# A pair begun in every step from step 165 on, chunks of two from batch 44, narrower load waits, allotment in pieces, fills over two steps

## The chip, the cores and the metric

The kernel runs on one core of a Trainium2 chip. A core has five engines that each work through their own list of instructions in order: PE (TensorE, matrix products), DVE (VectorE), ACT (ScalarE), POOL (GpSimd) and SP (SyncE, which here only issues transfers). The metric is the time of one execution on the device in microseconds; less is better.

## The reference

64 batches of 256 tokens, each of 256 numbers, go through two layers. The first is a graph attention with four heads and a linear layer; the second a graph attention with one head and a mixture of eight experts of which each token uses two. Each part is added to its input:

```
x = x + L0_gnn(layernorm(x), adj)        # 4 heads of 64, masked softmax over 256 nodes, elu
x = x + layernorm(x) @ weight.T + bias
x = x + L1_gnn(layernorm(x), adj)        # 1 head of 256, relu
t = layernorm(x)
rw, re = top_k(softmax(t @ router_w.T), 2); rw = rw / rw.sum()
x = x + t + sum over e of combine[:, e] * (gelu(t @ w1[e] + b1[e]) @ w2[e] + b2[e])
```

All arithmetic is in 32-bit floats.

## The kernel before

A batch is two tiles of 128 tokens. `batch_layers(b, ...)` carries one batch through both attentions and the linear layer, up to the router's logits. The last three batches (61 to 63) are computed **densely**: `route_dense` finds their two weights per token, and `dense_expert` runs each of the eight experts over all their tokens. The first 61 are **routed**: they are gathered into chunks, and when the last batch of a chunk is done, `route` does the following for the whole chunk.

1. `top_two` finds each token's two experts, and two matmuls (L1099, L1100) with a running sum give every token-expert couple a row in that expert's region of a table in HBM, `xs`. This is a chain of small DVE operations.
2. `allot` decides from the counts how many blocks of 256 rows (a **pair**, two tiles) are full in each expert's region, and which expert and which block each of the next `n` pairs takes. It is a generator in five pieces, 19 DVE operations in all (L833 to L870). `in_one` runs all the pieces at once; `spread`, true for chunks of four batches, takes one piece in each of four steps.
3. `send` scatters the rows of each tile to `xs`, twice, once for each expert (L1056, indirect transfers issued by POOL).
4. The pairs are put into the list `waiting`.

After the last chunk, `allot` is called once more for the blocks that are not full (`FLUSH` = 14 pairs), and eight **fills** (L1168, issued by SP) write harmless rows behind each expert's last row.

`expert_pair` is one pair: four loads of its rows from `xs` into `xr` (L892), one of four further numbers per row into `xt` (L903), one of the expert's weights into `we` (L917); DVE turns the rows into `sT` (L117); `hidden` multiplies with the first weights (`ph`, L950) and applies gelu; `result` multiplies with the second (`py`, L965), DVE adds the bias (`y`, L975), and ACT scales each row (L943). Then `scatter` adds the two tiles of `y` to the output with two indirect transfers from POOL (L986). Rows of different pairs can be the same token, so both adds of a pair wait until the two adds of the pair before have landed.

What a load waits for: `xs` is one tensor, so a load of it waits for every earlier write of `xs`, sends and fills alike, that nothing has waited for yet. It also waits explicitly for the transfers in `needs`, the sends of its own chunk (or the fills). Sends and fills themselves are exempt from waiting for loads and for each other (the group "rows").

The order of all instructions is written by the loop at the end of the function. It counts **steps**, three to a batch (`TICKS` = 3); batch b begins at step 3b. In each step every active generator is advanced to its next `yield`, in the order of the numbers that they yielded last, smaller first; a negative number means once more in the same step. Up to step 176 two pairs are begun in every third step; from `DRAIN_AT` (step 177) on, one in each step, as long as fewer than three results wait for `scatter`. One `scatter` is issued per step. A dense expert's job is begun as soon as it is ready, one per step for the first dense batch and one per two steps for the other two. The same constant `DRAIN_AT` also sets one number of `batch_layers`, which the change leaves alone. The last store, of batch 63, waits for all the adds (`store_dense`, L1031).

Of the kernel before, what the change touches and what calls it, by code (L numbers as in the profile page):

```python
# [17 lines left out]
SYNC = mybir.DependencyQuery.ANY_SYNC  # L18
# [9 lines left out]
def kernel(  # L28
# [18 lines left out]
    B, N, D = x.shape  # L47
# [4 lines left out]
    NT = N // P  # L52
# [4 lines left out]

    CHUNKS = (4,) * 12 + (2,) * 5 + (1,) * 3  # L60
    ROUTED = sum(CHUNKS)
    DENSE = B - ROUTED
    assert DENSE > 0
# [298 lines left out]

    half_done = []
    DRAIN_AT = TICKS * (B - 5)
    order, order_steps = [], []

    def norm_stats(src):
# [407 lines left out]
    def in_one(parts):  # L775

        got = None
        for got in parts:
            pass
        return got  # L780
# [95 lines left out]
    def expert_pair(j, n, ids, ef, regs, needs):  # L876

        i = j % GROUP
        upto = min(j + GROUP, n)
        if i == 0:  # L880
            _, regs["e"] = nc.values_load_multi_w_load_instructions(
                ids[0:1, 0, j:upto], engines=[mybir.EngineType.SP], min_val=0, max_val=E - 1,
                skip_runtime_bounds_check_because=WHY,
            )
            _, regs["t"] = nc.values_load_multi_w_load_instructions(
                ids[0:1, 1, j:upto], engines=[mybir.EngineType.SP], min_val=0, max_val=E * CAP,
                skip_runtime_bounds_check_because=WHY,
            )
        e_sp, t_sp = regs["e"][i], regs["t"][i]
        xr = io.tile([P, PAIR // S, KT * S], F32, tag="xr", name="xr", bufs=XBUFS)  # L890
        loads = [
            nc.sync.dma_start(  # L892
                out=xr[g * S : (g + 1) * S],
                in_=xs_d.rearrange("(t c q) f -> t q c f", c=PAIR // S, q=S)[
                    bass.ds(t_sp, 1), :, :, g * KT * S : (g + 1) * KT * S
                ].rearrange("t q c f -> (t q) c f"),
            )
            for g in range(P // S)
        ]

        xt = small.tile([P, 2, ROW - D], F32, tag="xt", name="xt", bufs=14)
        loads.append(
            nc.sync.dma_start(  # L903
                out=xt,
                in_=xs_d.rearrange("(t k p) c -> t p k c", p=P, k=2)[
                    bass.ds(t_sp, 1), :, :, D:
                ].rearrange("t p k c -> (t p) k c"),
            )
        )
        for load in loads:  # L910
            tc.add_to_no_dep_group("rows", load.ins)
            for name in needs:
                tc.add_manual_dep(
                    load.ins, name, AFTER, reason="any sent row may lie in the pair"
                )
        we = io.tile([P, WROW], F32, tag="we", name="we", bufs=WBUFS)
        nc.sync.dma_start(  # L917
            out=we, in_=wpack[bass.ds(e_sp, 1), :, :].rearrange("e p c -> (e p) c")
        )
        yield 90  # L920

        yield 95 if more else 75
        xT = turned(work.tile([P, KT, PAIR], F32, tag="sT", name="sT", bufs=3), xr)
        w = small.tile([P, 2], F32, tag="w", name="w", bufs=12)
        yield 30
        yield 30
        hT = hidden(xT, we)
        yield -65
        nc.vector.scalar_tensor_tensor(
            w[:, :, None], xt[:, :, 1:2], ef[:, j : j + 1], xt[:, :, 2:3],  # L930
            op0=ALU.is_equal, op1=ALU.mult,
        )
        nc.vector.tensor_tensor(w[:, :, None], w[:, :, None], xt[:, :, 3:4], ALU.add)
        yield 80
        if i == 0:
            _, regs["x"] = nc.values_load_multi_w_load_instructions(
                ids[0:1, 0, j:upto], engines=[mybir.EngineType.PE, mybir.EngineType.DVE],
                min_val=0, max_val=E - 1, skip_runtime_bounds_check_because=WHY,
            )
        y = result(hT, bass.ds(regs["x"][i], 1))  # L940
        yield 2
        for t in range(2):
            nc.scalar.activation(y[:, t, :], y[:, t, :], AF.Copy, scale=w[:, t : t + 1])  # L943
        scatters.append((y, xt))
# [109 lines left out]
    def send(xe, at):  # L1054

        d = nc.gpsimd.indirect_dma_start(  # L1056
            out=xs_d[: E * CAP * PAIR, :],
            out_offset=bass.IndirectOffsetOnAxis(ap=at, axis=0), in_=xe, in_offset=None,
        )
        tc.declare_no_dep(  # L1060
            d.ins, query=SYNC, group="rows", reason="sent rows are all different, and none is in a full pair"
        )
        tc.add_to_no_dep_group("rows", d.ins)
        sent.append(d.ins.name)
        nc.gpsimd.nop()

    def later(rank, *phases):
# [5 lines left out]
    def route(c, row0, nt, n, last, xng, lg):  # L1073
# [60 lines left out]
        for i, xe in enumerate(xng):  # L1134
            vec.tensor_copy(xe[:, :, D + 1 :], tail[:, i * NT : (i + 1) * NT, :])
        parts = allot(c, n, False)
        if n and not spread:
            ids, ef = in_one(parts)
        if last:
            ends_at = rt([E], "ends_at", 2, I32)  # L1140
            vec.tensor_copy(ends_at, rows[0])
# [2 lines left out]
        for t in range(nt):  # L1144
            for k in range(2):
                send(xng[t // NT][:, t % NT, :], pos[:, k, t : t + 1])
            if n and spread and t in (1, 2, 4, 5):
                ids, ef = next(parts) or (None, None)
            if not last:
                yield 95  # L1150
            elif t % 2:
                yield 95
        needs = sent[mark:]
        if n:
            regs = {}
# [2 lines left out]
            )  # L1158
        if last:
            parts = allot(c + 1, FLUSH, True)  # L1160
            ids2, ef2 = in_one(parts)
            _, ends_sp = nc.values_load_multi_w_load_instructions(
                ends_at[0:1, :], engines=[mybir.EngineType.SP], min_val=0,
                max_val=(E * CAP - 1) * PAIR, skip_runtime_bounds_check_because="rows of a region",
            )
            filled = []
            for e in range(E):
                d = nc.sync.dma_start(  # L1168
                    out=xs_d[bass.ds(ends_sp[e], PAIR), :].rearrange("(p t) c -> p t c", t=2),
                    in_=fill,  # L1170
                )
                tc.declare_no_dep(
                    d.ins, query=SYNC, group="rows", reason="filling rows lie behind an expert's last row"
                )
                tc.add_to_no_dep_group("rows", d.ins)
                filled.append(d.ins.name)
                nc.sync.nop()
            yield 95
            regs2 = {}
            waiting.extend(  # L1180
                lambda j=j: expert_pair(j, FLUSH, ids2, ef2, regs2, filled)
                for j in range(FLUSH)
            )
# [53 lines left out]
    with tc.manual_schedule():  # L1237
        while more or active or waiting or dense_jobs or scatters:
            phase = step % TICKS
            if more and (phase == 0 or step == 2):  # L1240
                nxt = next(batches, None)
                more = nxt is not None
                if more:
                    begin(nxt, 40 if phase == 0 else 25)
            if step >= SETUP_AT and setup:
                begin(setup.pop(0)(), 90)
            if step >= DRAIN_AT:
                if waiting and len(scatters) < 3:
                    begin(waiting.pop(0)(), 90)
            elif phase == 1:  # L1250
                credit = min(credit + 3.0, 2.0)
                while waiting and credit >= 1.0:
                    credit -= 1.0
                    begin(waiting.pop(0)(), 90)
            if dense_jobs and step >= dense_free:
                units, job = dense_jobs.pop(0)
                dense_free = step + units
                begin(job(), 90)
            if scatters:
                def one():  # L1260
                    scatter()
                    return
                    yield
                begin(one(), 97)
            order_steps.append(step)
            queue = [(a[0], a[1], a) for a in active]
            heapq.heapify(queue)
            while queue:
                *_, entry = heapq.heappop(queue)
                entry[0] = next(entry[2], None)  # L1270
                if entry[0] is not None and entry[0] < 0:
                    entry[0] = -entry[0]
                    heapq.heappush(queue, (entry[0], entry[1], entry))
            if half_done:
                finish_norms(NT)
            if half_squared:
                finish_squares()
            active[:] = [a for a in active if a[0] is not None]
            step += 1
# [35 lines left out]
```

## Time and profile before

| | |
|---|---|
| median of 3 runs | 1519.05 us (1517.03 to 1519.11) |
| profiled execution | 1516.68 us |
| its span, first to last instruction | 1514.9 us |
| granted TensorE clock, mean | 0.985 |
| busy: PE, PEld, DVE, ACT, POOL | 1421.4, 1261.2, 1245.9, 1017.4, 875.8 us |
| indirect adds L986 | 258, 1604 ns each |
| indirect sends L1056 | 244, 1089 ns each |
| matmuls of the experts, L950 and L965 | 1032 + 192 and 1224 |
| loads of `xr`, `xt`, `we` (pairs) | 516, 129, 129 |

PEld is the loading of weights into TensorE, which runs beside its products. A busy engine is one that executes an instruction; waiting and the issuing of transfers do not count. [...] In a line of the timeline come the start and the duration in microseconds, engine, line, operation, what is written and read, and in brackets the idle time of the engine before it and what ended that.

### The profile page before, as it was taken

The page shows a single profiled execution, that of the slowest core. Times are in us where ns is not written, and L with a number is a line of the kernel's source. Part 1 is how long each engine was busy: PE and PEld are TensorE (multiplying, and loading weights), DVE is VectorE, ACT ScalarE, POOL GpSimd, SP SyncE. Part 2 cuts the span into 40 slices and gives each one's busy share as a digit, 9 for nine tenths or more (in the row PEclk, how much of TensorE's full clock was granted, in tenths as well). Part 3 has the DMA queues.
Part 4 walks back from the last instruction along what each step waited for, and adds up shares of the span by engine and source line. Part 5 has one row for each costly group of instructions (what it writes and reads, how often), then busy time and mean ns, then how long its engine had stood idle before and what let it go on. Part 6 is the DMA issues. An engine that isn't in the chain of part 4 may idle for free. (4 is left out here: it accounts for less than half of the span.)

```text
span 1514.9 us, 29999 instructions
## 1 busy us (share of the span) xinstructions
PE 1421.4 (94%) x8134; PEld 1261.2 (83%) x8134; DVE 1245.9 (82%) x4419; ACT 1017.4 (67%) x2396; POOL 875.8 (58%) x845
## 2 busy tenths in 40 slices
PE   7899999999999999999999999998899989699992
PEld 6698888789898989999998989997788877578881
DVE  7689999989898889888898989899888878654541
ACT  1477667677778777777777777776678779553330
POOL 2122546455858586767676676756747776544444
PEclk9999999999999999999999999999999999999996
DMA  4822334576878788787877787867768676797743
GB/s 129 244 91 73 117 103 139 134 178 158 198 154 192 162 194 171 170 183 166 181 181 164 175 185 160 187 156 166 172 154 186 132 162 128 174 208 156 142 65 52
DMA packets 354355, 236.38 MB, mean 156 GB/s; under 512 B 246276, under 2 KB 316428, under 8 KB 354188
## 3 DMA queue, kind: packets, MB, share of 16 engines
q1 hardware_dynamic: 301272, 158.16, 41.7%
q0 software_dynamic: 48864, 66.33, 24.3%
q10 hardware_dynamic: 4052, 9.98, 2.1%
q8 instruction: 67, 1.10, 0.3%
q14 instruction: 100, 0.82, 0.2%
HBM read 146.00 MB, written 88.35 MB: 155 GB/s over the span
## 5 line engine op out<-in xcount | busy, mean ns | idle before, releaser
L986 POOL DMA_INDIRECT out_dram<-y,xt x258 | 413.9, 1604 | 195.7 <-issue 66.6
L585 PE MATMUL pv<-q,z 128*128 128x65 f32 (+1 forms) x2560 | 362.6, 296 | 0.4
L585 PEld LDWEIGHTS pv<-q,z 128*128 128x128 f32 x2560 | 329.9, 193 | 13.0 <-DVE z L571 1.1
L1056 POOL DMA_INDIRECT xs<-xng,pos x244 | 265.7, 1089 | 65.4 <-issue 59.8
L965 PE MATMUL py<-w2s,hT 128*128 (+1 forms) x1224 | 280.6, 380 | 6.3 <-ACT hT L956 6.3
L965 PEld LDWEIGHTS py<-w2s,hT 128*128 128x128 f32 x1224 | 228.3, 190 | 38.3 <-ACT hT L956 9.1
L950 PE MATMUL ph<-sT,we 128*128 128x256 f32 x1032 | 244.2, 387 | 14.9 <-DMA we<-wpack 8.8
L571 DVE SCALAR_TENSOR_TENSOR z<-z,q,mask 128x256 f32<-128x256 f32 x504 | 231.5, 482 | 14.7 <-DMA z<-terms 5.7
L950 PEld LDWEIGHTS ph<-sT,we 128*128 128x128 f32 x1032 | 198.0, 194 | 43.6 <-issue 10.3
L460 ACT COPY xT<-pt 128x512 f32<-128x512 f32 x209 | 121.3, 588 | 99.2 <-PE pt L454 76.6
L943 ACT ACTIVATE y<-y,w 128x256 f32<-128x256 f32 x258 | 112.9, 498 | 110.2 <-DVE y L975 93.6
L956 ACT ACTIVATE hT<-ph,we 128x256 f32<-128x256 f32 x306 | 123.9, 473 | 63.0 <-PE ph L950 42.4
L407 POOL TENSOR_SCALAR rstd<-mv 128x4 f32<-128x4 f32 (+1 forms) x66 | 15.6, 236 | 248.1 <-DVE mv L380 194.7
L425 ACT ACTIVATE off<-x,sums 128x256 f32<-128x256 f32 x256 | 129.4, 505 | 7.9 <-DVE x L668 1.7
L505 PE MATMUL pq<-wx,xT 128*128 128x259 f32 x512 | 125.3, 387 | 9.6 <-ACT xT L460 6.9
L470 PE MATMUL pq<-wx,xT 128*128 128x268 f32 x512 | 128.1, 394 | 1.5 <-ACT xT L460 0.7
L975 DVE TENSOR_TENSOR y<-py,b2s 128x512 f32<-128x512 f32 x129 | 85.9, 685 | 52.4 <-PE py L965 39.4
L661 PE MATMUL pf<-wfT,xT 128*128 128x256 f32 x512 | 122.7, 383 | 0.0
L505 PEld LDWEIGHTS pq<-wx,xT 128*128 128x128 f32 x512 | 94.3, 189 | 30.2 <-ACT xT L460 13.5
L470 PEld LDWEIGHTS pq<-wx,xT 128*128 128x128 f32 x512 | 97.8, 192 | 20.7 <-DVE wx L168 1.3
L689 ACT ACTIVATE rel<-pv,rinv 128x256 f32<-128x256 f32 x128 | 54.4, 470 | 84.5 <-DVE rinv L592 53.8
L661 PEld LDWEIGHTS pf<-wfT,xT 128*128 128x128 f32 x512 | 93.8, 193 | 10.4 <-issue 0.2
(174 smaller groups left out, 2383.7 us busy)
## 6 DMA issues: line engine op xcount, KB each, us to landing
we<-wpack SPq DMA_DIRECT2D x145, 288.0 KB
xr<-xs SPq DMA_DIRECT2D x516, 64.0 KB
z<-terms SPq DMA_DIRECT2D x46, 512.0 KB
xin<-in_x_dram SPq DMA_DIRECT2D x64, 256.0 KB
out_dram<-base SPq DMA_DIRECT2D x61, 256.0 KB
xblk<-in_x_dram SPq DMA_DIRECT2D x188, 64.0 KB
z<-terms ACTq DMA_DIRECT2D x17, 512.0 KB
out_dram<-y,xt POOLq DMA_INDIRECT x258
```

The costliest lines, as they stand in the source:

```text
L425: nc.scalar.activation(off, src[:, t, :], AF.Square, bias=sums[:, t : t + 1], scale=-float(D), accum_out=sq[:, at + t : at + t + 1],)
L460: nc.scalar.copy(dst, pt)
L470: nc.tensor.matmul(pq.rearrange("p h c -> p (h c)"), xT[:, k, t * P : (t + 1) * P], wx[:, k, :], start=(k == 0), stop=(k == KT - 1),)
L505: nc.tensor.matmul(pq, xT[:, k, t * P : (t + 1) * P], wx1[:, k, :], start=(k == 0), stop=(k == KT - 1),)
L571: nc.vector.scalar_tensor_tensor(z[:, j, :, h, :], terms, q[:, j, h, HD + 2 : HD + 3], masks[0][:, j, :].rearrange("p (t i) -> p t i", t=N ...
L585: nc.tensor.matmul(pv[:, h, :], z(j, h, t), q[:, j, h, : d + 1], start=(j == 0), stop=(j == NT - 1),)
L661: nc.tensor.matmul(pf[:, t, :], xT[:, k, t * P : (t + 1) * P], wfT[:, k, :], start=(k == 0), stop=(k == KT - 1),)
L950: nc.tensor.matmul(ph[:, f, :], we[:, k * D + f * P : k * D + (f + 1) * P], xT[:, k, :], start=(k == 0), stop=(k == KT - 1),)
L956: nc.scalar.activation(hT[:, f, :], ph[:, f, :], AF.Gelu, bias=we[:, C_B1 + f : C_B1 + f + 1])
L965: nc.tensor.matmul(py[:, t, :], hT[:, f, t * P : (t + 1) * P], w2s[:, e, f * D : (f + 1) * D].rearrange("p e c -> p (e c)"), start=(f == 0 ...
L986: d = nc.gpsimd.indirect_dma_start(out=out_rows, out_offset=bass.IndirectOffsetOnAxis(ap=xt[:, t, 0:1].bitcast(I32), axis=0), in_=y[:, t, ...
L1056: d = nc.gpsimd.indirect_dma_start(out=xs_d[: E * CAP * PAIR, :], out_offset=bass.IndirectOffsetOnAxis(ap=at, axis=0), in_=xe, in_offset=None,
```

## The change

- Chunks: eleven of four batches, seven of two and three of one, where there were twelve, five and three. The batches 44 to 47 become two chunks. There are 61 routed batches as before.
- From step 165 on (`SINGLE_AT`) one pair is begun in each step; two in every third step before that. `DRAIN_AT` stays for the number in `batch_layers`.
- A load waits only for the sends of its own chunk; for the pairs of the last call of `allot`, for the fills. Sends and fills are put in a group "sent", from which all loads are exempt apart from `needs`.
- In chunks of two and of one, and in the last call, `allot` runs a piece at a time: one beside each of the four tiles' sends for two batches, two beside each of the two tiles' sends for one batch, and one beside every second fill.
- The last chunk sends one tile per step (it sent its two tiles in one step), and the eight fills are issued in two steps, four in each.

```diff
-    CHUNKS = (4,) * 12 + (2,) * 5 + (1,) * 3
+    CHUNKS = (4,) * 11 + (2,) * 7 + (1,) * 3
...
     DRAIN_AT = TICKS * (B - 5)
+    SINGLE_AT = TICKS * (B - 9)
...
         for load in loads:
+            tc.declare_no_dep(
+                load.ins, query=SYNC, group="sent", keep=needs,
+                reason="the pair's rows were sent by these or by sends that earlier loads waited for",
+            )
             tc.add_to_no_dep_group("rows", load.ins)
-            for name in needs:
+            for ins in needs:
                 tc.add_manual_dep(
-                    load.ins, name, AFTER, reason="any sent row may lie in the pair"
+                    load.ins, ins.name, AFTER, reason="any row of these may lie in the pair"
                 )
...
         tc.add_to_no_dep_group("rows", d.ins)
-        sent.append(d.ins.name)
+        tc.add_to_no_dep_group("sent", d.ins)
+        sent.append(d.ins)
...
         parts = allot(c, n, False)
-        if n and not spread:
-            ids, ef = in_one(parts)
+        turns = (1, 2, 4, 5) if spread else (0, 1, 2, 3) if nt == 2 * NT else (0, 0, 1, 1)
...
-            if n and spread and t in (1, 2, 4, 5):
+            for _ in range(turns.count(t) if n else 0):
                 ids, ef = next(parts) or (None, None)
-            if not last:
-                yield 95
-            elif t % 2:
-                yield 95
+            yield 95
...
             parts = allot(c + 1, FLUSH, True)
-            ids2, ef2 = in_one(parts)
...
             for e in range(E):
+                if e % 2 == 0:
+                    ids2, ef2 = next(parts) or (None, None)
                 d = nc.sync.dma_start(
...
                 tc.add_to_no_dep_group("rows", d.ins)
-                filled.append(d.ins.name)
+                tc.add_to_no_dep_group("sent", d.ins)
+                filled.append(d.ins)
                 nc.sync.nop()
-            yield 95
+                if e % 4 == 3:
+                    yield 95
...
-            if step >= DRAIN_AT:
+            if step >= SINGLE_AT:
                 if waiting and len(scatters) < 3:
                     begin(waiting.pop(0)(), 90)
```

## The prediction

> **What bounds the kernel now.** I read the page's busy shares first, then busy time by stage (the table of windows), because an average over 1515 us hides four different stages. Columns: the window, its length, busy time of PE, PEld, DVE, ACT, POOL with instruction counts, granted clock, DMA share, GB/s.
>
> ```profile
> 303.00:1006.00 703.00, 702.53 (x4168) 633.93 (x4167) 630.88 (x2158) 536.90 (x1268) 477.24 (x451) 1.00 0.79 176
> 1006.00:1102.00 96.00, 84.10 (x481) 73.92 (x480) 83.96 (x330) 62.99 (x149) 65.64 (x64) 0.98 0.71 164
> 1102.00:1201.00 99.00, 95.76 (x541) 84.20 (x540) 85.44 (x320) 75.62 (x164) 60.15 (x55) 1.00 0.71 157
> 1201.00:1320.00 119.00, 105.48 (x537) 89.40 (x535) 96.56 (x468) 94.94 (x197) 78.29 (x68) 0.97 0.72 154
> 1320.00:1340.00 20.00, 10.85 (x45) 9.12 (x46) 6.64 (x20) 8.14 (x16) 9.31 (x7) 0.83 0.83 192
> 1340.00:1470.00 130.00, 129.97 (x602) 114.09 (x601) 67.98 (x168) 51.17 (x116) 55.80 (x37) 1.00 0.72 139
> 1470.00:1515.00 45.00, 16.97 (x75) 13.58 (x74) 9.93 (x21) 4.89 (x12) 18.69 (x13) 0.75 0.37 50
> ```
>
> PE is full to 1006 and from 1340 to 1470; there only less work on PE helps. PE loses 12 us at 1006 to 1102, 3 in the next stage, 14 in the next, 9 at 1320 to 1340 and 28 in the last 45 us. The first loss is DVE's: 87% busy on average, and it runs the allotment's 19 small operations in one lump. The timeline of DVE shows one such lump from 1080.15 to 1083.68; a few microseconds later PE stands 4.47 us for DVE at 1092, and 2.92 us at 1043 after the lump that ended at 1036.
>
> Then the timeline of SP (start, duration, instruction) and the waits of PE between 1318 and 1340:
>
> ```profile
> 1311.63 5.93 SPq L1168 DMA_DIRECT2D xs<-fill  x8
> 1321.58 1.93 SPq L892 DMA_DIRECT2D xr<-xs  x4
> ...
> 1328.32 0.36 SPq L1008 DMA_DIRECT2D we<-wpack  x1
> ```
> ```profile
> PE ph L950 <- DMA we<-wpack: 8.8, 1, 8.8
> ```
>
> Eight fills take SP 5.9 us, and the next pair's load, though its rows are not filling rows, stands until they have landed (in the chain of waits, "1316.81 4.57 DMA xs<-fill"). All weights and loads behind it are late, and PE stands 8.8 us.
>
> Last, the timeline of POOL in the tail, and of ACT where the last pair's y is ready:
>
> ```profile
> 1466.78 1.54 POOL L986 DMA_INDIRECT out_dram<-y,xt  x1 [3.12 <-ACT hT L956]
> 1468.63 1.54 POOL L986 DMA_INDIRECT out_dram<-y,xt  x1 [0.31 <-issue]
> 1473.19 1.54 POOL L986 DMA_INDIRECT out_dram<-y,xt  x1 [3.01 <-ACT hT L956]
> ...
> 1504.88 1.54 POOL L986 DMA_INDIRECT out_dram<-y,xt  x1 [2.91 <-DMA out_dram<-y,xt]
> ```
> ```profile
> 1474.90 0.91 ACT L943 ACTIVATE y<-y,w 128x256 f32<-128x256 f32 x2 [1.67 <-DVE y L975]
> ```
>
> A pair's two adds wait for the landing of the pair's before, so this chain goes no faster than 6.4 us a pair (1473.19 - 1466.78). The last y is ready at 1475.8, its add starts 29.1 us later at 1504.88, and the span ends 10 us after that. Pair 96 (counted from 0) had y at 1256.9 and its add at 1276.22: 19.3 us, the lag of an unblocked chain. So the chain fell behind after 1276, and the end is set by it: the last dense matmul ends at 1488.8, and DVE's last sums some 3 us later, at about 1492.
>
> **What the Trainium skill says.** "DMA: Bandwidth & Descriptors", Anatomy of one DMA: a semaphore wait happens on the issuing sequencer before dispatch. The trace agrees: weights behind the waiting load were late. The same section gives about 2.0 us fixed per GpSimd DMA, mostly the write's receipt; here the adds take 3.6 us from the end of issue to landing (chain: "1475.04 3.56 DMA out_dram<-y,xt"), and I use that. "VectorE: DVE Perf Modes", The TRN2 errata: each operation pays a fixed latency whatever its size. Here 128x8 takes 0.17 us and 128x512 0.65, so a route of two batches costs nearly what one of four does.
>
> **The change part by part.** From the loop's rules and the order of the built program: pairs begun by the end of step 164 are 73 in both; step 176, 81 before and 85 after; step 191, 96 and 100; step 206, 111 and 113; all 129 by step 224 before, 222 after. The list runs empty at steps 192 and 197, so four pairs gained become two. A batch begins every third step; its first L470 matmul dates the stages: batch 51 at 926.1, 55 at 1006.4, 59 at 1102.5, 63 at 1200.9.
>
> *Steps 153 to 164 (batches 51 to 54), 80.3 us now.* One route more in all: 58 DVE instructions, 3 PE, 7 ACT, 2 SP; sends, loads and adds stay 244, 516 and 258. The next four batches, which now hold two routes of two batches at the same two pairs a batch, take 96.1: +15.8 is the upper end. The lumps behind the two PE stalls (2.92 + 4.47) are cut in four, each piece beside sends, which I take to save half. POOL gets four sends in each of steps 159 to 162, as it does now in 171 to 174, where it is busy 17.6 us of 21.7 and 18.5 of 27.1. I take +8; ends 0 (DVE keeps pace, as at its 90% before 1006) and +16.
>
> *Steps 165 to 176, 96.1 us now.* Four more pairs, each 16 matmuls of 216 ns, 3.46 us of PE, and 1.8 us of DVE (0.70 + 0.69 + 0.21 + 0.16). Batches 59 to 62 are this very mix, uncut lumps included, and took 98.4; less 2.4 for the lumps is 0. Ends -4 and +7 (all the DVE time uncovered).
>
> *Steps 177 to 191.* Pairs as before; lumps cut: -2, ends -5 and +3.
>
> *Steps 192 to 206 (about 1225 to 1337).* Two pairs fewer, 6.9 us of PE, of which I count 3, as PE is not full there. The narrower wait lets pairs of the last chunks load between the fills, which go out four in each of two steps at 0.7 us: of the 9 us stall I take 7. Waits for their own sends remain, with weights and dense work queued behind them on SP; a load lies some 20 to 29 us ahead of its matmuls here (1200.0 to 1229.0), which covers the longest such wait seen, 9.2. The last chunk's sends take one step more, covered by pairs still waiting. -10; ends -16 and -2.
>
> The narrower wait is worth nothing before: by SP's waits, loads stood 93.2 us for sends between 303 and 1006 while PE was full. The lists of instructions instead of names cost nothing.
>
> *The tail, from step 207.* A step is 32 matmuls, 6.9 us of PE. The last pair begins two steps earlier: -13.8 for its y. The lag of its add should fall from 29 to about 20, as the starved steps let the chain catch up: -9, together -23. A cap: from step 206, 25 adds remain now and took 1329.4 to 1504.9, 7.0 each; 23 remain after, at 6.9 about 159, that is -16, and about -4 for a chain that is less late at step 206. I take -18; ends -10 and -23. Dense work then ends at about 1492 - 4 - 7 = 1481, before the last add has landed.
>
> Sum: 8 + 0 - 2 - 10 - 18 = -22. The profiled execution took 1516.68 (its span 1514.9), so 1494.7; the median of the three runs is 2.4 higher: **1497**.
>
> **Rivals.** *DVE takes over (slower).* Place: steps 153 to 176. If the added route costs its full 15.8, the four pairs their 7 uncovered, the later stages give back only 7, and the chain stays behind so that the tail gives 13: 16 + 7 - 7 - 13 = +3, 1522; with gaps on top as in 1075 to 1102 (27.1 us for a batch) about 1526. It decides once batches 51 to 58 take over 20 us more than now. For it: 87 to 94% DVE there. Against: DVE at 90% before 1006 leaves PE full.
>
> *The chain stays behind.* The fills' stall stops PE, not the chain of adds, which ran through it at 7 to 9 us a pair. If it is still late at step 206, only two pairs are saved, 12.9, against +6 to +8 early and -4 between: -10, 1509.
>
> *The waits come back.* With an empty list, loads go out right behind their own sends; three chunks at up to 9.2 us on SP eat some 15 of the 22: 1512. That the narrow wait does nothing in the built program is this case too.
>
> **How the numbers follow.** The forecast has 0.55, the chain 0.20, the waits 0.10, DVE 0.15. A measurement tells about 0.2% (3 us) from no change. Of DVE's 0.15, 0.12 is slower and 0.03 the same; 0.02 more of "same" comes from the waits. Faster 0.83, same 0.05, slower 0.12. Low end 1478: the tail's -23 and half of the other gains beyond the forecast. High end 1519: the chain and the waits within it.
>
> **What would show it.** Right: PE's 8.8 us wait for weights at the fills gone; lag of the last add near 20; batches 51 to 58 within 12 us of 176.4; last pair's y about 18 us earlier. Wrong: batch 59's L470 later than 1122, or the adds' chain back to back from step 200 on.

## The result and the profile after

The changed kernel takes 1508.2 us (median of 5 runs, 1503.2 to 1509.4), the kernel before beside it 1517.0 (1512.0 to 1519.1): **ratio 0.9933, 95% interval 0.9909 to 0.9957**. It is faster, and inside the range of the forecast, but by 9 us where the forecast had 22. The range, 1478 to 1519, reached up to the time of the kernel before, so that lying inside it says little; the terms tell more. The profiled execution took 1509.41 us, its span 1507.6. (The median of before differs a little between chips: 1516.5, 1516.9 and 1519.3 beside the experiments below, so ratios are compared.)

Busy time by stage of the kernel after; the windows are set by the same events as those of before (batches 20, 55, 59 and 63 begin with the first four), so they start later:

```profile
307.00:1025.00 718.00, 707.78 (x4172) 635.51 (x4171) 639.98 (x2231) 538.45 (x1271) 484.37 (x459) 1.00 0.75 172
1025.00:1124.00 99.00, 94.11 (x537) 83.22 (x536) 85.41 (x318) 75.16 (x164) 60.09 (x56) 1.00 0.79 176
1124.00:1222.00 98.00, 96.52 (x545) 85.04 (x544) 86.36 (x321) 77.92 (x171) 65.83 (x61) 1.00 0.77 165
1222.00:1310.00 88.00, 76.15 (x392) 64.96 (x391) 69.58 (x340) 70.56 (x146) 61.15 (x56) 0.94 0.72 153
1310.00:1330.00 20.00, 17.18 (x84) 13.66 (x83) 15.96 (x83) 11.98 (x26) 13.67 (x11) 1.00 0.96 249
1330.00:1470.00 140.00, 131.99 (x610) 114.44 (x609) 75.63 (x219) 61.01 (x135) 59.94 (x39) 1.00 0.71 135
1470.00:1508.00 38.00, 25.32 (x112) 20.26 (x110) 14.22 (x30) 6.86 (x16) 15.57 (x10) 0.94 0.35 50
```

The second line shows what was bought: 99 us in place of 96 for batches 55 to 58, but with 537 matmul records instead of 481 and PE idle for 5 us instead of 12. The fifth shows the fills: PE idle 3 us of 20 instead of 9. The first shows the surprise: PE was idle 0.5 us of 703 there, and is now idle 10 us of 718. Part of that is the added route in batches 51 to 54, but from 345 to 905 us, ahead of it, PE is busy 555.50 of 560 us instead of 559.57. In time, each batch's first projection matmul (L470, now L471) dates the stages:

| stage, us | before | after | difference | forecast |
|---|---|---|---|---|
| to the start of batch 51 | 926.1 | 937.1 | +11.0 | 0 |
| batches 51 to 54 | 80.3 | 87.7 | +7.4 | +8 |
| 55 to 58 | 96.1 | 99.0 | +2.9 | 0 |
| 59 to 62 | 98.4 | 98.0 | -0.4 | -2 |
| from batch 63 to the span's end | 314.0 | 285.8 | -28.2 | -10 and -18 |
| span | 1514.9 | 1507.6 | -7.3 | -22 |

The timeline of SP at the fills, after (start, duration, instruction), answers to the fence of before with its x8:

```profile
1315.60 2.41 SPq L1171 DMA_DIRECT2D xs<-fill  x4
1318.29 2.79 SPq L893 DMA_DIRECT2D xr<-xs  x4
1321.27 0.40 SPq L904 DMA_DIRECT2D xt<-xs  x1
1322.17 0.11 SPq L922 DMA_DIRECT2D we<-wpack  x1
1322.90 2.41 SPq L1171 DMA_DIRECT2D xs<-fill  x4
1325.42 0.64 SPq L1013 DMA_DIRECT2D we<-wpack  x1
```

A pair's loads stand between the two groups and follow the first by 0.3 us, where before the next load followed the last of eight fills by 4.0 us. The prediction put those 4.0 us down to the landing of the fills, and PE's stall with them; the trace of before shows more. Within the 4.0 us, SP spends 2.6 on two loads of registers (L881 and L885, 1.30 and 1.25 us; in the kernel after, none is at this place), and waits 1.1 for the fills. And SP was late already when it came to the fills: ahead of the pair before them it had stood 9.2 us for sends. SP's waits of before from 1290 to 1345 (total us, times, longest):

```profile
SPq L892 <- DMA xs<-xng,pos: 12.8, 2, 9.2
SPq L892 <- DMA xs<-fill: 1.1, 1, 1.1
```

After, PE's waits from 1180 to the end hold no wait for `we` any more; the longest are

```profile
PE py L970 <- ACT hT L961: 10.3, 10, 3.3
PE pt L455 <- DVE x L669: 7.5, 2, 4.4
```

The tail: the timelines of ACT, for the last pair's y, and of POOL, for the last adds:

```profile
1475.81 0.91 ACT L948 ACTIVATE y<-y,w 128x256 f32<-128x256 f32 x2 [1.67 <-DVE y L980]
```
```profile
1484.51 1.56 POOL L991 DMA_INDIRECT out_dram<-y,xt  x1 [3.00 <-DMA out_dram<-y,xt]
1486.37 1.56 POOL L991 DMA_INDIRECT out_dram<-y,xt  x1 [0.30 <-issue]
1490.85 1.56 POOL L991 DMA_INDIRECT out_dram<-y,xt  x1 [2.92 <-DMA out_dram<-y,xt]
1492.71 1.56 POOL L991 DMA_INDIRECT out_dram<-y,xt  x1 [0.30 <-issue]
1497.86 1.56 POOL L991 DMA_INDIRECT out_dram<-y,xt  x1 [3.59 <-issue]
```

The last y is ready at 1476.7, and its first add starts at 1497.86: a lag of 21.1 us instead of 29.1. The chain of adds still sets the end, as the last store's wait on SP shows:

```profile
SPq L1036 <- DMA out_dram<-y,xt: 7.2, 1, 7.2
```

But it does so by little. DVE's last sums of the dense experts end at 1500.3 and the wait for the adds at 1503.6; before, it was 1490.7 and 1510.5.

### The profile page after: what moved, and what is told of

It is laid out like the page before. It is cut to its first block, busy times and chain, and to the rows that moved or that the text cites. A ratio compares the mean times of both kernels' runs of the same rounds, so it can differ in the third digit from the quotient of the medians.

```text
span 1507.6 us, 30029 instructions
## 1 busy us (share of the span) xinstructions
PE 1429.0 (95%) x8138; PEld 1263.9 (84%) x8138; DVE 1252.7 (83%) x4476; ACT 1024.6 (68%) x2403; POOL 870.2 (58%) x845
## 5 line engine op out<-in xcount | busy, mean ns | idle before, releaser
L1061 POOL DMA_INDIRECT xs<-xng,pos x244 | 259.5, 1064 | 65.3 <-issue 60.3
L970 PE MATMUL py<-w2s,hT 128*128 (+1 forms) x1224 | 283.5, 382 | 11.5 <-ACT hT L961 10.3
L506 PE MATMUL pq<-wx,xT 128*128 128x259 f32 x512 | 128.8, 394 | 18.6 <-ACT xT L461 16.9
L471 PE MATMUL pq<-wx,xT 128*128 128x268 f32 x512 | 127.1, 391 | 2.8 <-DVE xT L117 1.6
L471 PEld LDWEIGHTS pq<-wx,xT 128*128 128x128 f32 x512 | 97.5, 191 | 21.9 <-DVE xT L117 1.8
```

What stands on the lines that cost most here:

```text
L471: nc.tensor.matmul(pq.rearrange("p h c -> p (h c)"), xT[:, k, t * P : (t + 1) * P], wx[:, k, :], start=(k == 0), stop=(k == KT - 1),)
L506: nc.tensor.matmul(pq, xT[:, k, t * P : (t + 1) * P], wx1[:, k, :], start=(k == 0), stop=(k == KT - 1),)
L970: nc.tensor.matmul(py[:, t, :], hT[:, f, t * P : (t + 1) * P], w2s[:, e, f * D : (f + 1) * D].rearrange("p e c -> p (e c)"), start=(f == 0 ...
L1061: d = nc.gpsimd.indirect_dma_start(out=xs_d[: E * CAP * PAIR, :], out_offset=bass.IndirectOffsetOnAxis(ap=at, axis=0), in_=xe, in_offset=None,
```

## The experiments

Times of stages in the table at the end come from the profiled run of each kernel, one execution each. "21 to 50" is from the start of batch 21 to the start of batch 50; the other columns go from the start of their first batch to the start of the batch after their last, or to the span's end. How far two such readings differ by chance can be seen in e3 and e5, whose instructions are in the same order up to the last fills: 89.8 and 87.5 us for batches 51 to 54. So differences of 2 to 3 us in one stage of one run are not read.

### The narrower waits: alone, late, and not at all

The forecast put the narrower wait at nothing while PE is full, and after was 11 us late just there, where no other edit acts yet. Three kernels try it. **e1_narrow_only** is the kernel before with these lines alone:

```diff
         for load in loads:
+            tc.declare_no_dep(
+                load.ins, query=SYNC, group="sent", keep=needs,
...
-        sent.append(d.ins.name)
+        tc.add_to_no_dep_group("sent", d.ins)
+        sent.append(d.ins)
...
```

> The kernel before with the narrower load waits alone. Theory A (the waits are worth nothing while PE is full, and the changed kernel's 11 us of delay up to batch 50 came by chance, from a lowered clock): batches 20 to 50 take 603 us in the profile as before, and the end comes 0 to 4 us earlier than before, since the adds' chain, not the stop of PE at the fills, sets it. Theory B (without the stop, SP runs ahead, its transfers fall elsewhere, and the full stage itself gets longer): batches 20 to 50 take about 609 us, and the time is 2 to 6 us above that of before.

Measured: ratio 1.002 (1.0003 to 1.0037). From the start of batch 20 to that of batch 50 it takes 609.3 us, the kernel before 602.9: theory B.

**e2_narrow_late** is the changed kernel, with narrow waits only for pairs begun from step 150 on:

```diff
+    LATE = TICKS * (B - 14)
...
-            tc.declare_no_dep(
+            if order_steps[-1] >= LATE:
+                tc.declare_no_dep(
...
```

> The changed kernel, with the narrow waits only for pairs begun from step 150 on; earlier loads wait for all sends, as before. Theory A: the same time as the changed kernel, ratio to before 0.993 within 0.002. Theory B: the full stage takes 603 us again from batch 20 to 50, and the time falls by about 6 us more, ratio to before about 0.989.

Measured: 0.989 (0.9861 to 0.9919), and 602.9 us from batch 20 to 50: theory B.

**e3_wide** is the changed kernel without `declare_no_dep`, all else kept:

```diff
-            tc.declare_no_dep(
-                load.ins, query=SYNC, group="sent", keep=needs,
...
-            )
```

> The changed kernel without the narrow waits at all: every load waits for all sends and fills issued before it. Theory A: 2 to 6 us slower than the changed kernel, because loads stand for the fills again and the last chunks' pairs for the newest sends, ratio 0.995 to 0.997. Theory B: the loss at the fills and the 6 us regained in the full stage cancel, ratio 0.992 to 0.994, with batches 20 to 50 at 603 us.

Measured: 1497.7 us, 0.9869 (0.9835 to 0.9903), the fastest kernel of this study and faster than either theory had it. Profiled span 1496.1. (The intervals of e2 and e3 overlap, so the two are not told apart.)

From the start of batch 21 to that of batch 50, every kernel with narrow waits there and the chunks of this stage unchanged takes 587.3 to 588.8 us (after, e1, e4, e7), every one with wide waits 582.3 to 583.8 (before, e2, e3, e5, e6, e8, e9, e10, e11). So the narrow waits cost some 5 us in the full stage, alone as within the change; in after, 4.1 of its 6.1 us more than before are idle time of PE. PE's waits from 345 to 905, first of before, then of after, then of e3 (line, what ended the wait, total us, times, longest):

```profile
PE pq L505 <- ACT xT L460: 0.3, 1, 0.3
```
```profile
PE pq L506 <- ACT xT L461: 3.8, 6, 0.8
PE pq L506 <- issue: 0.4, 1, 0.4
```
```profile
PE pq L506 <- ACT xT L461: 0.5, 2, 0.4
```

And what the wait was on SP, first before, then after:

```profile
SPq L622 <- DVE stats L379: 92.5, 19, 8.3
SPq L892 <- DMA xs<-xng,pos: 77.3, 14, 6.2
```
```profile
SPq L623 <- DVE stats L380: 208.7, 28, 9.1
```

The waits for sends are gone, as the change says. SP then arrives earlier at the next batch's input, whose buffer DVE frees: it stands there 28 times instead of 19, and for longer (208.7 us) than both waits took together (169.8). Nothing was gained for PE, and something was lost.

Nor do the narrow waits give anything back later: from batch 63 to the end e2 takes 283.8 us, e3 280.6. In the kernel before they do: e1 has no wait of PE for `we` from 1180 on either, and takes 4.5 us less from batch 63 to the end. In the changed kernel little is left to gain there: with wide waits, e3, PE's wait for `we` is 1.3 us.

### What carries the 5 us

In the narrow runs some small operations were seen to take longer. The timeline of e1 shows POOL's power at two times, and DVE beside the second:

```profile
358.91 1.04 POOL L448 TENSOR_TENSOR rstd<-rstd,mhalf 128x4 f32<-128x4 f32 x1
```
```profile
482.67 1.49 POOL L448 TENSOR_TENSOR rstd<-rstd,mhalf 128x4 f32<-128x4 f32 x1
```
```profile
482.56 0.69 DVE L652 TENSOR_TENSOR x1b<-x,bias_f 128x512 f32<-128x512 f32 x1
483.17 1.39 DVE L571 SCALAR_TENSOR_TENSOR z<-z,q,mask 128x256 f32<-128x256 f32 x3
```

The same operation takes 1.04 us at 358.91, beside small DVE operations, and likewise at 350.78, beside the bias add `y`, which reads one large operand from PSUM, where TensorE's products lie. It takes 1.49 here, beside operations with two large operands in SBUF, the core's working memory; others of this kind took up to 1.60. From the start of batch 21 to that of batch 50 it took over 1.3 us in 13 of 58 cases in e1 and 14 of 58 in after, against 8 of 58 both in before and in e3. It lies in the chain to `xT`. So two kernels compute half of these rstd on DVE: **e7_narrow_recip** from the changed kernel, **e8_wide_recip** from e3. Both leave out the square root, so their numbers are not the reference's, and they serve for times alone.

```diff
-        nc.gpsimd.tensor_scalar(
+        nc.vector.tensor_scalar(
             rstd[:, :n], sq[:, :n], 1.0 / D**3, EPS, op0=ALU.mult, op1=ALU.add
         )
-        nc.gpsimd.tensor_tensor(rstd[:, :n], rstd[:, :n], mhalf[:, :n], ALU.pow)
+        nc.vector.reciprocal(rstd[:, :n], rstd[:, :n])
```

> The changed kernel (narrow waits), with the second and the router's norm's rstd computed on DVE instead of POOL; the square root is left out (a reciprocal stands for the power, so that DVE gets two operations of 0.16 us for the two of POOL). It is a test of what carries the narrow waits' cost in the full stage (batch 21 to 50: 588.8 us narrow, 583.3 wide). Theory A, the cost is carried by POOL's power operation, which takes 1.49 to 1.60 us instead of 1.04 while DVE works on SBUF operands, and falls there more often with narrow waits: batch 21 to 50 takes at most 2 us more than in the run with wide waits and the same reciprocal. Theory B, the earlier transfers themselves delay PE in some other way: the difference stays at 4 to 7 us.

> The same reciprocal on DVE in the changed kernel with wide waits; it is the reference for the run before. PE is full in this stage in either case: batch 21 to 50 takes 582 to 584 us by both theories (583.3 with the power on POOL), as DVE has the room for 0.3 us more a half and the chain of a norm is 1 to 2 us shorter. The theories differ in the run before only: A at most 2 us above this one, B 4 to 7 us above.

Measured: 1.0094 (1.0061 to 1.0127) and 1.0039 (1.0017 to 1.0061). From batch 21 to 50: 587.4 and 582.3, a difference of 5.1 us. Theory B holds: the 29 powers that stay on POOL in that stage are all under 1.3 us, and the cost is all there. (Both are slower than their originals, mostly ahead of batch 21, which begins at 340.6 and 334.8 instead of 328.4 and 326.9.) The other slow operation, `by` (L709) at 0.43 instead of 0.16 us while POOL issues an add, came seven times in that stage in e1 and six in after, once each in before and e3, and not in e7, so it isn't the carrier either. **What delays the copies that PE waits for is open**; shown are the edit that brings the delay, the place and the size.

### One pair per step

**e4_single177** is the changed kernel with one pair a step from step 177 on, as before: `SINGLE_AT = TICKS * (B - 5)`.

> The changed kernel with one pair per step only from step 177 on, as before, and two per three steps up to there. If the gain comes from the two pairs taken out of the tail, this gives back about 10 us of chain of adds in the tail and saves 2 to 4 in batches 55 to 58: ratio to before 0.997 to 1.001. Rival (the list runs empty anyway, so the earlier start moves nothing that counts): ratio as the changed kernel's, 0.993.

Measured: 0.9984 (0.9968 to 1.0). Batches 55 to 58 take 86.3 us instead of 99.0; from batch 63 on it takes 302.3 instead of 285.8. The early pairs cost 12.7 us where they are put, and bring 16.5 at the end. The ratio is that of the first reading, and both sides are larger than it had them. The 12.7 is not a stall but work moved forward: PE is busy 94.1 us there instead of 81.8, as 11 pairs begin on it instead of 8.

### The chunk split in two

**e9_wide_chunks12** is e3 with `CHUNKS = (4,) * 12 + (2,) * 5 + (1,) * 3`.

> The changed kernel with wide load waits, and with batches 44 to 47 as one chunk of four as before. Theory A, the split is what feeds one pair per step from step 165 on: without it the list of waiting pairs runs empty between chunks, pairs begin later, and the tail gives back 5 to 12 us: ratio 0.990 to 0.995 (1502 to 1510 us), against 0.9869 with the split. Theory B, as the first term of the forecast reads, the split only adds a route (+8 us in batches 51 to 54) and one pair per step could do without: batches 51 to 54 take 2 to 8 us less than the 89.8 of the kernel with it, and the ratio is 0.982 to 0.986.

Measured: 0.998 (0.9963 to 0.9998). Batches 51 to 54 take 80.0 instead of 89.8, so the split costs what the forecast said and a little more. But by the first matmul of batch 59 only 81 pairs have begun on PE, as in before, against 84 in e3; by batch 63 it is 93 against 96. From batch 63 to the end it takes 303.8 us instead of 280.6. That is theory A, the list being empty when a pair could be begun, but far dearer than its range: the tail gives back 23 us, not 5 to 12. Besides, batches 55 to 58 take 6.7 us more than in e3, with three pairs fewer: PE is idle there for 13.5 us instead of 4.0, and the granted clock is 0.95 instead of 1.00. What makes PE stand there was not tested.

### The allotment in pieces

**e6_wide_lump** is e3 with the lumps back. The first chunk of two and the last allotment keep their pieces, and a lump stands beside the first tile's sends, a step later than in before. (`allot` yields four times, so its pieces are four, not five as said at the start.) On all engines but DVE the order of instructions is that of e3.

```diff
-        turns = (1, 2, 4, 5) if spread else (0, 1, 2, 3) if nt == 2 * NT else (0, 0, 1, 1)
+        turns = (1, 2, 4, 5) if spread else (0, 1, 2, 3) if c == 11 else (0, 0, 0, 0)
```

> The changed kernel with the old, wide load waits, and with the allotment of the chunks of two (but the first of them) and of one run in one lump at the first tile's sends, as before. Theory A, as in the forecast: PE stands behind the lumps of DVE as it did before at 1043 (2.92 us) and 1092 (4.47 us); cutting them saved about half there and 2 us in steps 177 to 191, so batches 51 to 58 take 190 to 193 instead of 187.7, and the time is 3 to 8 us above 1497.7 (ratio 0.989 to 0.992). Theory B, PE would have waited for another DVE operation in any case: within 2 us of 1497.7 (ratio 0.9855 to 0.9883).

Measured: 0.9982 (0.9965 to 0.9999), some 17 us more than e3, twice the upper end of theory A. Batches 55 to 58 take 8.0 us more, 59 to 62 4.9, and from batch 63 on 3.7. Of the 8.0, 4.8 are idle time of PE; in the rest it is busy for longer, at a granted clock of 0.97 instead of 1.00.

**e10_before_pieces** is the other way round, the kernel before with the pieces alone (its last allotment stays one lump):

```diff
-        if n and not spread:
-            ids, ef = in_one(parts)
+        turns = (1, 2, 4, 5) if spread else (0, 1, 2, 3) if nt == 2 * NT else (0, 0, 1, 1)
...
-            if n and spread and t in (1, 2, 4, 5):
+            for _ in range(turns.count(t) if n else 0):
...
```

> The kernel before with one part of the change alone: the allotment of the chunks of two and of one runs a piece beside each tile's sends instead of in one lump. Only DVE's order of instructions changes. Putting the lump back into the changed kernel cost some 17 us of its time. Theory A, the lumps stop PE in the kernel before as well, whatever else changes: ratio 0.987 to 0.992 (1497 to 1505 us). Theory B, they cost much only beside the added route and pairs, when DVE has no room left; in the kernel before, the two stalls of PE that they leave (2.92 and 4.47 us) are all there is to save, and the tail's chain of adds hides part: ratio 0.994 to 0.999 (1508 to 1515 us).

Measured: 0.9938 (0.9911 to 0.9964): as much as the whole change. Batches 55 to 58 fall from 96.1 to 88.5 us. PE's waits between 1000 and 1110, first of before, then of e10:

```profile
PE pt L454 <- DVE x L695: 4.5, 1, 4.5
PE ph L950 <- DVE sT L117: 2.9, 1, 2.9
PE pq L505 <- ACT hT L956: 1.9, 1, 1.9
```
```profile
PE pq L505 <- ACT xT L460: 2.2, 2, 1.4
PE pq L505 <- issue: 1.9, 1, 1.9
```

Both stalls behind DVE are gone, not halved. Of the 7.6 us of this stage, 5.8 are idle time of PE (6.1 us instead of 11.9). The other 1.8 are busy time, for the same number of matmuls: in before the clock was granted at half just behind the stall of 4.47 us, which ended at 1092.3, while in e10 it is 1.00 in the whole stage. From 1093 to 1096 in before (columns as above; the clock is the third number from the end):

```profile
1093.00:1096.00 3.00, 3.00 (x9) 2.46 (x8) 2.82 (x6) 2.90 (x6) 2.39 (x3) 0.50 1.00 157
```

The tail adds 4.3 us, and PE's wait for weights at the fills falls from 8.8 to 1.3, though the fills still go out in one step. The ratio lies just outside theory B's range, and its interval reaches into both; the two stalls of this stage are B's account, the gain in the tail is in neither. Beside the added route and pairs such lumps cost 17 us (e6), which B had said as well.

### The fills in one step

**e5_wide_fills1** is e3 with the eight fills in one step and the last allotment ahead of them in one lump (`if e == 0: ids2, ef2 = in_one(parts)`, and the `yield` at the last fill).

> The changed kernel with the old, wide load waits, and besides with the eight fills issued in one step as before (all pieces of the last allotment ahead of them). Against the same kernel with the fills in two steps, whose PE waits 1.3 us for weights around the fills and which takes 0.9869 of the time of before (1497.7 us). Theory A, the two steps are what removed PE's 8.8 us stall: a load issued behind eight fills stands until they have landed, the weights behind it are late, PE waits 5 to 9 us for we again, and the time is 1502 to 1506 (ratio 0.990 to 0.993). Theory B, one pair per step had already put enough loads ahead: PE waits under 3 us for we, the time is 1496 to 1500 (ratio 0.986 to 0.9885).

Measured: 0.9906 (0.9881 to 0.993). The timeline of SP, and PE's waits from 1300 to 1345, e5 and then e3:

```profile
1321.65 5.67 SPq L1167 DMA_DIRECT2D xs<-fill  x8
1331.34 1.93 SPq L893 DMA_DIRECT2D xr<-xs  x4
```
```profile
PE ph L951 <- DMA we<-wpack: 3.6, 1, 3.6
```
```profile
PE ph L951 <- DMA we<-wpack: 1.3, 1, 1.3
```

Theory A by the time, though the interval overlaps with e3's; PE's own wait, 3.6 us, lies between the two theories. The account of theory A does not hold as it was told: a load waits for fills in both kernels, 3.8 us behind eight in e5 and 3.3 behind the first four in e3 (SP's waits). What the second step changes is that four fills go out behind that pair's loads and weights: the dense expert's weights (L1009) are issued 12.9 us after the first fill in e5 and 10.9 in e3. What the last allotment's lump has to do with it was not tested apart.

### Going further

**e11_wide_s153** is e3 with `SINGLE_AT = TICKS * (B - 13)`; **e12_wide_c10_s153** has besides ten chunks of four and nine of two.

> A candidate: the changed kernel with wide load waits and one pair begun per step from step 153 on instead of 165. Theory A, what is left to gain is the adds' lag (18 us behind the last y at 1468.3): pairs begun earlier let the chain start earlier, and PE's idle time after 1190 (12 us to 1320) is filled less but the end comes 3 to 6 us sooner, ratio 0.983 to 0.985. Theory B, DVE has no room for four more pairs in batches 51 to 54, PE stands there 4 to 8 us more, and the list runs empty sooner, so nothing comes back: ratio 0.987 to 0.992.

> The same candidate with one more chunk of four split into two chunks of two (batches 40 to 43), so that the pairs come earlier. Theory A: the list no longer runs empty early, 1 to 3 us less than the run before, ratio 0.981 to 0.984. Theory B: one more route costs DVE 58 instructions in batches 47 to 50, where PE is full and DVE at 90%, another 8 to 10 us as batches 51 to 58 cost, ratio 0.990 to 0.996.

Measured: 1.0004 (0.9983 to 1.0024) and 0.9993 (0.9972 to 1.0015). All of e3's gain is lost. In e11, batches 51 to 58 take 207.4 us instead of 187.7, and the stage from batch 63 on 281.9 instead of 280.6. In e12 the additional split adds 6.7 us between batch 21 and 50. Theory B by the time, and dearer than its upper end both times, but its reason is not shown. In batches 51 to 54 of e11 DVE is busy 81.2 of 102.7 us, or 79%, where in e3 it is 92%. PE's waits from 900 to 1130 name the copies to `xT` on ACT for 12.5 us, and the granted clock in batches 51 to 54 is 0.93 instead of 0.98. Nor do the pairs come much earlier: by batch 59, 85 have begun on PE, against 84 in e3.

Theory A of e11 had a flaw of its own. In e3 the last store finds the dense experts' sums done at 1491.9 and the adds landed at 1492.1. An earlier chain of adds alone could not have ended that kernel sooner.

| profiled run, us | 21 to 50 | 51 to 54 | 55 to 58 | 59 to 62 | 63 to end | span |
|---|---|---|---|---|---|---|
| before | 582.7 | 80.3 | 96.1 | 98.4 | 314.0 | 1514.9 |
| after | 588.8 | 87.7 | 99.0 | 98.0 | 285.8 | 1507.6 |
| e1 narrow only | 587.6 | 80.8 | 94.4 | 98.5 | 309.5 | 1515.1 |
| e2 narrow late | 582.9 | 87.6 | 99.8 | 97.8 | 283.8 | 1499.4 |
| e3 wide | 583.3 | 89.8 | 97.9 | 97.7 | 280.6 | 1496.1 |
| e4 single from 177 | 587.3 | 89.6 | 86.3 | 95.9 | 302.3 | 1510.7 |
| e5 wide, fills in one step | 583.6 | 87.5 | 98.4 | 97.9 | 288.4 | 1500.6 |
| e6 wide, lumps | 582.8 | 90.6 | 105.9 | 102.6 | 284.3 | 1511.2 |
| e9 wide, split undone | 583.4 | 80.0 | 104.6 | 98.3 | 303.8 | 1511.4 |
| e10 before, pieces | 583.8 | 80.0 | 88.5 | 97.7 | 309.7 | 1507.4 |
| e11 wide, single from 153 | 583.5 | 102.7 | 104.7 | 98.2 | 281.9 | 1514.4 |
| e12 wide, single from 153, ten fours | 590.0 | 103.7 | 99.2 | 96.7 | 281.0 | 1513.8 |

## Why the prediction was right, and where it was not

**The step that failed** is "The narrower wait is worth nothing before", that is, ahead of step 192. The argument was that loads stood 93 us for sends while PE was full, so that nothing could be gained; that a wait taken away could cost something was not weighed. It cost 6.1 us between batch 21 and 50 (5 in the pairs of kernels above). A further 4.9 of the 11.0 us arose ahead of batch 21; its start lies between 321.4 and 329.4 us in the runs of either kind but for the reciprocal's, 327.8 in e10 with wide waits, so this part is not put down to the change. Without the narrow waits the forecast's number would have been met: e3 takes 1497.7 us where 1497 was given, a ratio of 0.9869 where the forecast's is 0.9855. Not every term would: by the table e3 loses 4.6 us more than forecast in batches 51 to 62, starts batch 51 4.0 us late and gains 5.4 more behind batch 63; in part these cancel.

**Batches 51 to 54**, +8: +7.4, and e9 shows that it is the split: 80.0 without it, 87.5 to 90.6 in the kernels with it that begin single pairs from step 165 or later.

**Batches 55 to 58**, 0: +2.9, inside the ends, but as a sum of two larger terms than in the working. The lumps were worth 7.6 to 8.0 us there (e10, e6), not the 2.4 at which an uncut stage was discounted, and the early pairs cost 12.7 (e4), nearly all of it PE's own work on them. Reading the total from batches 59 to 62, "this very mix", worked because it held both.

**Batches 59 to 62**, -2: -0.4.

**The fills and the tail**, -28: -28.2. PE's stall for weights went as said, but not for the reason given. The reading had the fills' landing as its cause, and left out the 9.2 us that SP stood for sends just before. The narrow wait takes that wait away: in e1 the eight fills, still in one step, go out at 1299.1 instead of 1311.6, and PE does not wait for weights. Nor does that wait make the stall by itself: in e10 SP stands 9.5 us for sends at the same place, and the fills go out in one step, yet PE waits only 1.3 of the 8.8 us for weights. The change with wide waits left 3.6 with the fills in one step (e5) and 1.3 with two (e3). So the 7 us credited to the narrow wait would have come without it, and the tail's stage is as fast without it. From the start of batch 63 to the last y it is 254.9 us instead of 274.9, -20.0 where the terms gave -10 and -13.8; the lag went to 21.1 us, forecast about 20. That the total fits is in part luck: the y came less early than its terms had it, and the cap had taken 5 us off.

**The cap**, 23 adds at 6.9: from the first add of pair 105 (1332.7) to that of pair 128 (1497.9) it is 7.18 us a pair, 165 in all, not 159. The bound that it stood for held: adds end the kernel, by 3.3 us.

**The end of the dense work**, about 1481: 1500.3. The sum, 1492 - 4 - 7, left out the forecast's own +6 up to step 191; with it, it is 1487. Most of what is still missing is the 11.0 us of lateness at batch 51. So dense work is nearly as late as the adds, and in e3 it is as late: what was a bound far off has become the next one.

**The landing of an add**: the prediction has 3.6 us from the end of its issue. The 3.56 us of its chain begin at 1475.04, and there, by the timeline of POOL, the issue of the second add begins:

```profile
1475.04 1.54 POOL L986 DMA_INDIRECT out_dram<-y,xt  x1 [0.31 <-issue]
```

From the end of issue it is thus 2.0 us, and the difference that the prediction sees to the figure cited beside it falls away. No term of the sum used the 3.6; the 6.4 us a pair were measured as a whole.

**What would show it**: the wait for weights is gone and the lag near 20, as said; batches 51 to 58 took 186.7 us, 10.3 more than 176.4, within 12. The last y did not come 18 us earlier but 0.9 later; 11.0 of that are the lateness at batch 51. Batch 59 began at 1123.8, past the 1122 that was to tell of DVE; the mark was an absolute time and took in those 11.0 us, so it accused the wrong engine. A mark set on a difference between two events of the stage would not have.

**The rivals.** DVE's takeover did not decide: 10.3 us is short of the 20 given as its point. e11, with one pair a step from 12 steps earlier, passes that point, 31 us above before in batches 51 to 58, but with DVE less busy, so that it is not shown to be this rival. The chain's rival had 1509, and 1508.2 was measured; that is chance, as the tail gave its 28.2 us and the loss lies ahead of batch 59. The waits on sends did not come back: from 905 to 1440 us SP's waits name sends once, for 0.7 us, where before they held 38.9. Nor would they have done harm: e3 has 33.6 us of them and is the faster kernel.

## What to carry to other kernels

Removing a wait that hides behind a full engine is not free by that alone: what it held back now runs at another time, so test the edit alone and put it at a few us of either sign. Small operations in one lump on a busy engine (DVE was 87% busy there) cost as long as the engine beside it then stands, and here a stretch of half clock behind that; cutting the lumps, with no other engine's order touched, was worth 9 us (0.9938) alone and 17 within the change. Edits that feed each other (a split that brings work sooner, a loop that takes it sooner) are priced as one: undoing either of them gave back most of the gain. And when a chain that ends the kernel is shortened, look how far behind the next one is: here the adds' lead over the dense work fell from 20 us to 3.

## What the runs showed of the hardware that was not expected

POOL's 128x4 power took 1.04 us or 1.49 to 1.60 us, the longer ones beside DVE operations with two SBUF operands (1.49 in the fence above); a DVE operation of 0.16 us took 0.43 while POOL issued an add. Behind PE's stall of 4.47 us the clock was granted at 0.50 from 1093 to 1096; behind the one of 2.92 us it stayed at 1.00, from 1043 to 1050. From 345 to 905 us the DMA share was 0.79 and 0.80 in before and e3 and 0.75 and 0.76 in after and e1, with 175, 176, 172 and 174 GB/s moved: with narrow waits the packets took a smaller share of the time, and yet the kernel was slower.
